# Steps of the next layer's start placed anew in a twelve-layer decoder: keys a round sooner, first scores in the lead, one group inside the layer behind

## The chip, the cores and the metric

The kernel runs on one NeuronCore of a Trainium2 chip, as one program. The metric is the device time of one execution in microseconds (us); of the kernel before there are three runs, and their median counts. Engines in the text: PE (matmul; PEld its weight loads), DVE (vector), ACT (scalar functions), POOL (GpSimd), SP (which issues most transfers).

## The reference, cut to what matters

A decoder with four blocks; each has an attention, a cross attention to a context and a feed-forward part, every one with a layer norm ahead of it and a residual behind it. x is 32 sequences x 128 positions x 128 channels, in float32. So there are twelve layers:

```
x = x + layer(layernorm(x))          # for each of
0  state-space mixer
1  cross attention, 8 heads of 64
2  16 experts, 4 chosen per token
3  causal attention, 16 heads of 8; k, q and v from a latent of 64
4  cross attention, 16 heads of 8, with a key mask and biases
5  8 experts of width 256, 2 chosen; router: silu(x rw1 + rb1) rw2 + rb2
6  attention with one head of 128
7  cross attention, 16 heads of 8, plus a learned bias by relative position
8-11  sparsemax attention, a cross attention, experts
```

Every attention is softmax(q k^T * scale + terms) v, for each sequence by itself.

## The kernel before, in words

**Tiling.** x stays on the chip as eight groups of J = 4 sequences; a group is a tile of 128 positions x 4 x 128. Every layer loops over the eight groups (G = 8). In the attentions a round is one sequence, so a layer has 32 rounds, n = 4 g + j.

**Order of work.** Two things decide it. `Ordered` (L181) wraps PE, DVE and ACT; between `follow(T, A, V)` and `follow()` these engines keep the order of the program text. Outside it, and for POOL and SP always, a scheduler orders what has been written. Since `Ordered` makes the call, most rows of the profile have its line, L194, and are told apart by the names of their tiles. Layers are overlapped by generators: the steps of a coming layer are written as `yield`-separated pieces, and the running layer calls `next` on them at fixed places. `run2(lead3)`, `run3(lead5)`, `run5(bias7, lead7)` and `run7` at the bottom of the program chain them: layer 1 carries layer 2's `front(0)`, layer 2 carries the lead of layers 3 and 4 (which are one call of `attention16` with 64 rounds), these carry layer 5's, and so on.

**attention16** (L492-L622), for layers 3, 4 and 7. `scores(n)`: PE multiplies q by expanded keys into two PSUM tiles `two` (halves, 8 heads each; r = 0 to 3 are quarters of 4 heads), then adds the terms of `extra` (causal or mask) behind all four; DVE takes the maximum of each head (`s<-two`) and subtracts it into SBUF (`bbig<-two,s`). A head quarter with `own` = 1 is not subtracted: ACT's exponent reads PSUM itself, with the maximum as bias, a head at a time. `exponentials(half)` (called e(0), e(1)) are ACT's. `transposes(n, half)`: PE turns the exponents over, ACT copies them out. `weighted(n)`: PE multiplies by the values and by ones; DVE divides. `step(g)` runs the next piece of group g's preparation (norm, turning over, keys, queries, values; written in `layer3`, `layer4` and `layer7`). `expand_keys` (L467) multiplies k, copies it with ACT, and makes four masked copies `gbig<-bmid,cs` on POOL (L477), one for each r. `normed` (L386) is a layer norm whose products are POOL's (L397); `norm` (L334) uses DVE. In a round, `go_round` calls: transposes(n, 0); scores(n+1); transposes(n, 1); e(0); step of group g+1 (and of g+2 in the last round of a group); e(1); weighted(n-1); every fourth time `project`, which adds to x. `run` begins at n = -1, so the first scores of a call are made there. `lead` is five steps of group 0 and one of group 1.

**layer3**: the pieces of a group are the norm, the turning over, the latent (`a1_down`, round j = 1), k and q from the latent (round j = 2), and the values. **layer4**: `own` is (0, 0, 0, 0), scale 8^-0.5 is applied in the exponent.

**layer1** calls `next(then)` in its rounds n = 28 to 31. **layer2** and **layer5** are experts: `front(i)` is the router (norm, product, top choice by `first_k`, weights split in three parts); `by_expert` turns the weights over; `group(i, ...)` is the experts' matmuls. Layer 5's `group` interleaves pieces of `others` after each expert: for group i the one-head attention (layer 6) of group i-1, `one_head(i-1)`; for group 0 it is `bias7`, the splitting and spreading of layer 7's bias table. After group 7, `one_head(7)` runs by itself, interleaved with `lead7`.

Of the kernel before, what the change touches and what calls it, by code (L numbers as in the profile page):

```python
# [10 lines left out]
F32 = mybir.dt.float32  # L11
# [4 lines left out]
ALU = mybir.AluOpType  # L16
# [9 lines left out]
G = 8  # L26
# [178 lines left out]
def program(ctx, tc, cols, x, ctxt, mask, drop, dfirst, dsmall, dwide, drows, dunits, dexperts, dconst, drel, dwq, out):  # L205
# [286 lines left out]
    def attention16(*layers):  # L492
# [91 lines left out]
        def lead():  # L584
            for _ in range(5):
                step(0)
                yield
            step(1)
            yield

        def run(then):
            follow(T, A, V)
            for n in range(-1, groups * J + 2):
                go_round(n, then)
            follow()

        def go_round(n, then):
            g, j = n // J, n % J
            e = None
            if 0 <= n < groups * J:  # L600
                transposes(n, 0)
            if n + 1 < groups * J:
                e = scores(n + 1)
            if 0 <= n < groups * J:
                transposes(n, 1)
            if e:
                e(0)
            if n >= 0:
                step(g + 1)
                if j == 3:  # L610
                    step(g + 2)
                if g + 1 >= groups or (j == 3 and g + 2 == groups):
                    next(then, None)
            if e:
                e(1)
            if 0 < n <= groups * J:
                weighted(n - 1)
            if n > 1 and (n - 2) % J == J - 1:
                done = (n - 2) // J
                project(done % G, outs.pop(done), *layers[done // G][3:5])  # L620
# [12 lines left out]
    def linearT(w, src, bias=None, scale=1.0):  # L633

        p = ps()
        mm(p, w, src)
        o = gmid()
        if bias is not None:
            A.activation(o, p, AF.Identity, bias=bias)
        else:  # L640
            A.mul(o, p, scale)
        return o
# [311 lines left out]
    def layer1(then):  # L954
# [108 lines left out]
        for n in range(last + 1):  # L1063
            i, j = n // J, n % J
            ahead = n + 1 < last
            if n < last:
                if ahead:
                    e0 = scores(n + 1, 0)
                transposes(n, 0)
                if ahead:  # L1070
                    e0[0]()
            if n > 0:
                project_out(n - 1)
            if n < last:
                transposes(n, 1)
                if ahead:
                    e0[1]()
                    e1 = scores(n + 1, 1)
                if j == 1 and i + 1 < G:
                    prepare(i + 1, 1)  # L1080
                if n + 2 < last:
                    project_in(n + 2)
                if ahead:
                    e1[0]()
                    project_values(n + 1)
                    e1[1]()
                weighted(n)
                if j == 0 and 0 < i and i + 1 < G:
                    prepare(i + 1, 0)
                if i == G - 1:  # L1090
                    next(then)
        follow()

# [1 line left out]
    def layer2():  # L1095
# [4 lines left out]
        def front(i):  # L1100

            if i == 0:
                heads["w"] = part_tiles()
            wparts = heads["w"]
            xn = mid.tile([128, J, D], F32, tag="xn", name="xn", bufs=2)
            norm(xg[i], xn)
            yield
            xnT = turned_over(xn)
            yield
            lg = ps((128, J, 16))  # L1110
            for j in range(J):
                mm(lg[:, j, :], xnT[:, j * 128 : (j + 1) * 128], W["f0_gate"])
            sc, sf = small(J, 16), small(J, 16)
            A.activation(sc, lg, AF.Tanh, scale=0.5)
            V.tensor_scalar(sc, sc, 0.5, 0.5, ALU.mult, ALU.add)
            V.tensor_tensor(sf, sc, bc(WW["gate_bias"], 1, J), ALU.add)
            yield

            s4 = sf.rearrange("p j (g e) -> p (j g) e", e=4)
            pairs, gs = small(J * 4, 6), small(J, 4)  # L1120
            V.tensor_tensor(pairs[:, :, 0:3], s4[:, :, 0:3], s4[:, :, 1:4], ALU.add)
            V.tensor_tensor(pairs[:, :, 3:5], s4[:, :, 0:2], s4[:, :, 2:4], ALU.add)
            V.tensor_tensor(pairs[:, :, 5:6], s4[:, :, 0:1], s4[:, :, 3:4], ALU.add)
            V.tensor_reduce(gs.rearrange("p j g -> p (j g)"), pairs, AX.X, ALU.max)
            gm = first_k(gs, 4, 2)

            V.tensor_scalar(gm, gm, 1.0, -NEG, ALU.subtract, ALU.mult)
            V.tensor_tensor(s4, s4, bc(gm.rearrange("p j g -> p (j g)"), 2, 4), ALU.add)
            sel = first_k(sf, 16, 4)
            V.tensor_tensor(sel, sel, sc, ALU.mult)  # L1130
            tot = small(J)
            V.tensor_reduce(tot, sel, AX.X, ALU.add)
            V.tensor_scalar(tot, tot, 1e-20, None, ALU.add)
            V.reciprocal(tot, tot)
            V.tensor_scalar(tot, tot, 2.5, None, ALU.mult)
            V.tensor_tensor(sel, sel, bc(tot, 2, 16), ALU.mult)
            P.tensor_tensor(xg[i], xg[i], xn, ALU.add)
            heads[i] = xnT, part_weights(wparts[i % 2], sel, 16)
            yield
# [46 lines left out]
    def layer3():  # L1186
        def before(i, h):
            xn = normed(i)
            yield
            xnT = turned_over(xn)  # L1190
            yield
            p = ps()
            mm(p[0:64, :], W["a1_down"], xnT)
            lat = gmid((64, 512))
            A.copy(lat, p[0:64, :])
            yield
            h["k"] = expand_keys(W["a1_k"], lat)
            h["q"] = linearT(W["a1_q"], lat)
            yield
            v = values_tile()  # L1200
            pv, f = ps((128, J, 8)), small(J, 8)
            for j in range(J):
                mm(pv[:, j, :], lat[:, j * 128 : (j + 1) * 128], W["a1_v"])
            A.copy(f, pv)
            P.tensor_copy(diagonal(v)[:, 0:J], bc(f, 2, 4))
            h["v"] = lambda j, r, n: flat(v[:, j, n])

        return before, 8**-0.5, lambda i, j, r: ((identb, bc(causal, 1, 4), True),), W["a1_o"], None, None, (0, 0, 0, 1)


    def layer4():
        masks = {}

        def before(i, h):
            mi = gmid((128, J * S), I32)
# [6 lines left out]
            yield  # L1222
            h["k"] = expand_keys(W["x1_Wk"], ctxT[i], W["x1_bk"])
            yield
            h["q"] = linearT(W["x1_Wq"], xnT, W["L1_xattn_bq"])
            yield
            h["v"] = head_values(ctxT[i], W["x1_Wv"], WW["L1_xattn_bv"])

# [1 line left out]
            row = slice(32 * r, 32 * r + 1)  # L1230
            return ((onesb[row, :], bc(masks[i][row, j * S : (j + 1) * S], 1, 4), True),)

        return before, 8**-0.5, extra, W["x1_Wo"], WW["L1_xattn_bo"], None, (0, 0, 0, 0)


    def layer5():
# [3 lines left out]
        def front(i):  # L1240

            if i == 0:
                heads["w"] = part_tiles()
            wparts = heads["w"]
            xn = mid.tile([128, J, D], F32, tag="xn", name="xn", bufs=2)
            norm(xg[i], xn)
            yield
            xnT = turned_over(xn)
            yield
            if i == 0:  # L1250
                yield
                yield
            p = ps()
            mm(p, W["f1_rw1"], xnT)
            hT = gmid()
            A.activation(hT, p, AF.Silu, bias=W["L1_ffn_rb1"])
            lg = ps((128, J, 8))
            for j in range(J):
                mm(lg[:, j, :], hT[:, j * 128 : (j + 1) * 128], W["f1_rw2"])
            yield  # L1260
            l, m = small(J, 8), small(J)
            V.tensor_tensor(l, lg, bc(WW["L1_ffn_rb2"], 1, J), ALU.add)
            sel = first_k(l, 8, 2)
            V.tensor_reduce(m, l, AX.X, ALU.max)
            V.tensor_tensor(l, l, bc(m, 2, 8), ALU.subtract)
# [6 lines left out]
            heads[i] = xnT, part_weights(wparts[i % 2], sel, 8)  # L1272
            yield

        def run(first, then):
            ups = [U[5][:, e * 128 : (e + 1) * 128] for e in range(8)] + [U[6][:, e * 128 : (e + 1) * 128] for e in range(8)]
            downs = [U[6][:, 1024 + e * 128 : 1152 + e * 128] for e in range(4)]
            downs += [U[7][:, e * 128 : (e + 1) * 128] for e in range(12)]
            pick = picks(8)
            eb2 = W["f1_eb2"]  # L1280
            eb2_rest, eb2_parts = bmid((128, 128)), gmid((128, 3, 128), BF16)
            P.memset(eb2_rest, 0.0)
            V.tensor_copy(eb2_rest[0:24, :], eb2)
            parts3(eb2_rest, [eb2_parts[:, n] for n in range(3)])
            wT = by_expert(heads[0][1])
            for i in range(G):
                wT = group(i, wT, ups, downs, pick, eb2_parts, one_head(i - 1) if i else first)
            for _ in one_head(G - 1):
                next(then, None)

        def group(i, wT, ups, downs, pick, eb2_parts, others):
            xnT = heads.pop(i)[0]
# [17 lines left out]
            for e in range(8):  # L1310
# [5 lines left out]
                    for _ in front(i + 1):  # L1316
                        pass
                else:
                    next(others, None)
            for n in range(3):  # L1320
                mm(oT, eb2_parts[:, n], wT, False, n == 2)
            if i + 1 < G:
# [39 lines left out]
                V.scalar_tensor_tensor(xg[i][:, j, :], o[:, j, :], rec[:, j : j + 1], xg[i][:, j, :], ALU.mult, ALU.add)  # L1362
            yield

        return front(0), run


    def layer7():
# [501 lines left out]
    load_units(6, 7)  # L1870
    lead3, run3 = attention16(layer3(), layer4())
    run2(lead3)
    lead5, run5 = layer5()
    run3(lead5)
    load_units(8)
    bias7, layer = layer7()
    lead7, run7 = attention16(layer)
    run5(bias7, lead7)
    run7(iter(()))
    layer8_first()  # L1880
    layer9()

# [31 lines left out]
```

## Time and profile before

| | us |
|---|---|
| three runs: 3094.29, 3098.97, 3100.82; median | 3098.97 |
| the profiled execution, its own time | 3108.52 |
| its span in the profile | 3106.7 |
| layer 3, first to last reciprocal | 1134.4 to 1428.1 |
| layer 4, the same | 1435.6 to 1690.7 |
| layer 7, the same | 2086.5 to 2347.2 |
| layer 5's groups 1 to 6, each, by the ends of the additions to x | 43.2 |

Rows of a timeline give the start, the duration, the engine, the line, the operation, out<-in by tile names, the shape, how many instructions are joined in the row, and in brackets how long the engine had stood idle and which engine ended that. Rows of stretches give the busy time of each engine, and PEclk, the granted clock as a share of full speed (mean over the whole profile: 0.903). A wait is put down to the engine that released it last.

### The profile page before, as it was taken

The numbers are of one execution on the slowest core, as the hardware profiler recorded it, in microseconds if no ns is written. First come the engines' busy times: TensorE is split into PE (matmuls) and PEld (weight loads), VectorE is DVE, ScalarE is ACT, GpSimd is POOL, SyncE is SP. The second block draws the span as 40 slices with busy tenths as digits, with TensorE's granted clock in tenths as the row PEclk, the third lists the DMA queues.
The fourth block names the chain that finished last, engine by engine and source line by source line (L and its number), as shares of the span: only waits on it lengthen the run. The fifth ranks groups of instructions, "written<-read, shape, count | busy, mean of one in ns | idle before, by whom it ended". The sixth has DMA issues, their size and how long they took to land.

```text
span 3106.7 us, 55574 instructions
## 1 busy us (share of the span) xinstructions
PE 2576.8 (83%) x22554; PEld 1651.8 (53%) x22554; DVE 2106.3 (68%) x4228; ACT 1509.0 (49%) x3411; POOL 996.4 (32%) x1034
## 2 busy tenths in 40 slices
PE   4887889999989988888887999978886869886554
PEld 2555556777744445556664444445553657543433
DVE  4776747888788756667877555458895328777883
ACT  3555534444422245556654445447772226555563
POOL 3343332322210122234542000034434355424444
PEclk8888879999989999999999999979997889997777
DMA  3000000000000000000000000000003243100000
GB/s 108 2 2 2 5 19 4 8 8 1 11 11 1 0 31 2 5 8 9 8 5 15 1 1 1 0 1 2 1 2 125 79 150 106 62 18 14 21 11 21
DMA packets 50146, 68.35 MB, mean 22 GB/s; under 512 B 3681, under 2 KB 41570, under 8 KB 49762
## 3 DMA queue, kind: packets, MB, share of 16 engines
q1 hardware_dynamic: 42608, 33.84, 3.5%
q0 software_dynamic: 6848, 27.81, 2.7%
q8 instruction: 178, 2.92, 0.4%
q10 hardware_dynamic: 434, 3.14, 0.3%
q14 instruction: 78, 0.64, 0.1%
HBM read 51.11 MB, written 13.68 MB: 21 GB/s over the span
## 4 chain that ended last, share of the span: by engine, by line
PE 51%; DVE 30%; ACT 7%; POOL 7%; issue 3%; DMA 1%; another core or an unknown queue 1%; SPq 0%; POOLq 0%; DVEq 0%; ACTq 0%
PE ps L194 22%; PE two L194 15%; PE acc L194 14%; DVE bbig L194 12%; DVE s L194 9%; DVE bmid L194 4%; DVE gmid L194 3%; ACT bbig L194 3%; POOL xn L397 3%; POOL gbig L477 2%; ACT bmid L194 2%; POOL s L395 1%; ACT gmid L194 1%; ACT gbig L194 1%; DVE x L194 1%
## 5 line engine op out<-in xcount | busy, mean ns | idle before, releaser
L194 PE MATMUL ps<-cs,bbig 128*128 128x128 f32 x2208 | 330.9, 290 | 77.8 <-ACT bbig L194 43.4
L194 ACT COPY bbig<-ps 128x512 f32<-128x512 f32 x416 | 226.9, 586 | 270.3 <-PE ps L194 270.0
L194 PEld LDWEIGHTS ps<-cs,bbig 128*128 128x128 f32 x2208 | 255.9, 147 | 183.7 <-ACT bbig L194 98.0
L194 DVE TENSOR_REDUCE s<-two 128x8 f32<-128x1024 f32 (+1 forms) x192 | 234.2, 1220 | 143.5 <-PE two L194 142.4
L194 PE MATMUL two<-xnT,u 128*128 128x512 f32 x512 | 264.5, 617 | 14.0 <-DVE bmid L194 7.8
L194 DVE TENSOR_TENSOR bbig<-bbig 128x256 f32<-128x256 f32 (+4 forms) x394 | 274.3, 749 | 2.0 <-ACT bbig L194 1.0
L194 PE MATMUL acc<-bmid,u 128*128 128x512 f32 x448 | 238.5, 619 | 29.6 <-DVE bmid L194 28.2
L194 PE MATMUL two<-gbig,gmid 32*128 32x512 f32 (+1 forms) x1280 | 205.9, 578 | 32.9 <-POOL gbig L477 32.0
L477 POOL TENSOR_SCALAR gbig<-bmid,cs 128x512 f32<-128x512 f32 x96 | 148.6, 1564 | 209.0 <-ACT bmid L194 209.0
L194 DVE TENSOR_TENSOR bmid<-bmid,ps 128x512 f32<-128x512 f32 x192 | 129.9, 684 | 109.1 <-ACT bmid L194 90.3
L194 ACT ACTIVATE bbig<-bbig 128x1024 f32<-128x1024 f32 (+1 forms) x160 | 141.8, 887 | 94.7 <-DVE bbig L194 94.2
L194 ACT ACTIVATE bbig<-two,s 128x256 f32<-128x256 f32 (+1 forms) x384 | 153.9, 439 | 26.9 <-DVE s L194 23.5
L194 ACT ACTIVATE bmid<-two 128x512 f32<-128x512 f32 x104 | 61.7, 596 | 196.3 <-PE two L194 186.4
L194 PEld LDWEIGHTS two<-xnT,u 128*128 128x128 f32 x512 | 92.6, 194 | 119.1 <-issue 55.2
L194 PEld LDWEIGHTS acc<-bmid,u 128*128 128x128 f32 x448 | 80.7, 195 | 130.2 <-DVE bmid L194 72.6
L194 DVE TENSOR_TENSOR bbig<-two,s 128x1024 f32<-128x1024 f32 (+1 forms) x128 | 139.7, 1092 | 8.6
L194 ACT ACTIVATE bmid<-two,ws 128x512 f32<-128x512 f32 x128 | 85.2, 686 | 117.7 <-PE two L194 115.8
L1014 POOL TENSOR_TENSOR bbig<-bbig,s 128x1024 f32<-128x1024 f32 x32 | 60.6, 1893 | 238.6 <-PE two L194 154.4
L194 ACT ACTIVATE bbig<-bbig,s 128x128 f32<-128x128 f32 x384 | 118.8, 388 | 24.2 <-DVE s L194 24.2
L194 PE MATMUL ps<-cs,xn 128*128 128x128 f32 x288 | 66.2, 318 | 72.8 <-ACT xn L194 31.4
L489 POOL MEMSET val<- 128x512 f32 x72 | 39.0, 543 | 260.8 <-PE acc L194 260.0
L194 PEld LDWEIGHTS two<-gbig,gmid 32*128 32x128 f32 (+1 forms) x1280 | 82.0, 191 | 73.9 <-POOL gbig L477 35.2
(291 smaller groups left out, 5976.9 us busy)
## 6 DMA issues: line engine op xcount, KB each, us to landing
u<-in_units SPq DMA_DIRECT2D x10, 768.0 KB
gmid<-in_ctx SPq DMA_DIRECT2D x16, 256.0 KB, 2.6
xs<-bbig SPq DMA_DIRECT2D x4, 903.0 KB, 6.0
xt<-xs SPq DMA_DIRECT2D x28, 129.0 KB, 3.0
x<-in_x SPq DMA_DIRECT2D x8, 256.0 KB, 10.6
gmid<-in_mask SPq DMA_DIRECT2D x8, 256.0 KB, 3.3
ys<-bbig SPq DMA_DIRECT2D x2, 1024.0 KB
gmid<-ys SPq DMA_DIRECT2D x8, 256.0 KB, 5.3
```

Source lines behind the costliest of these rows:

```text
L194: d = f(*args, **kwargs)
L395: P.tensor_tensor(rs, rs, K["nhalf"], ALU.pow)
L397: P.tensor_scalar(xn[:, j, :], xg[i][:, j, :], mv[:, j, 0:1], rs[:, j : j + 1], ALU.subtract, ALU.mult)
L477: P.tensor_scalar(o[:, n, :], k, K["n4"][:, n : n + 1], None, ALU.mult)
L489: P.memset(o, 0.0)
L1014: (V if c2 else P).tensor_tensor(pr[:, four, :], pr[:, four, :], bc(nm[:, four], 2, 256), ALU.mult)
```

## The change

- **Layer 3**: for groups 1 to 7, k and q become a function `late`, kept in `held`, and `go_round` calls it at the end of the round in which the latent is made, after `weighted`.
- **attention16**: `lead` gets a seventh piece, scores(0) with both exponentials; `run` starts at n = 0. `go_round` also calls `next(others)` in each round, after `weighted`.
- **Layer 4**: q is scaled by 8^-0.5 when it is copied (its bias once, in front); the scale of the scores is 1.0; `own` is (0, 0, 0, 1).
- **Layer 1** calls `next(then)` at n = 27 to 30.
- **Layers 2 and 5**: `front(0)` uses `normed`. In layer 5's `front(0)` Silu is replaced by Identity, Tanh and a product on DVE, with the router logits halved in turn; its two empty pieces go; the picks and the parts of the output bias (`setup`) move from `run` into the lead.
- **Layers 5 to 7**: `bias7` runs in group 1 beside `one_head(0)`, `lead7` in group 7 beside `one_head(6)`, and `one_head(7)` is given to `run7` as `others`.

```diff
@@ attention16
             step(1)
             yield
+            e = scores(0)
+            e(0)
+            e(1)
+            yield
 
-        def run(then):
+        def run(others, then):
             follow(T, A, V)
-            for n in range(-1, groups * J + 2):
-                go_round(n, then)
+            for n in range(groups * J + 2):
+                go_round(n, others, then)
             follow()
...
             if 0 < n <= groups * J:
                 weighted(n - 1)
+            if g + 1 < groups and "late" in held[g + 1]:
+                held[g + 1].pop("late")()
+            next(others, None)
@@ linearT
-            A.activation(o, p, AF.Identity, bias=bias)
+            A.activation(o, p, AF.Identity, bias=bias, scale=scale)
@@ layer1
-                if i == G - 1:
+                if n in range(last - 5, last - 1):
                     next(then)
@@ layer2
-            xn = mid.tile([128, J, D], F32, tag="xn", name="xn", bufs=2)
-            norm(xg[i], xn)
+            if i == 0:
+                xn = normed(i)
+            else:
+                xn = mid.tile([128, J, D], F32, tag="xn", name="xn", bufs=2)
+                norm(xg[i], xn)
@@ layer3
-            yield
-            h["k"] = expand_keys(W["a1_k"], lat)
-            h["q"] = linearT(W["a1_q"], lat)
+
+            def late():
+                h["k"] = expand_keys(W["a1_k"], lat)
+                h["q"] = linearT(W["a1_q"], lat)
+
+            if i:
+                h["late"] = late
+            yield
+            if i == 0:
+                late()
             yield
@@ layer4
+        V.tensor_scalar(W["L1_xattn_bq"], W["L1_xattn_bq"], 8**-0.5, None, ALU.mult)
...
-            h["q"] = linearT(W["x1_Wq"], xnT, W["L1_xattn_bq"])
+            h["q"] = linearT(W["x1_Wq"], xnT, W["L1_xattn_bq"], 8**-0.5)
...
-        return before, 8**-0.5, extra, W["x1_Wo"], WW["L1_xattn_bo"], None, (0, 0, 0, 0)
+        return before, 1.0, extra, W["x1_Wo"], WW["L1_xattn_bo"], None, (0, 0, 0, 1)
@@ layer5
-            if i == 0:
-                yield
-                yield
             p = ps()
             mm(p, W["f1_rw1"], xnT)
             hT = gmid()
-            A.activation(hT, p, AF.Silu, bias=W["L1_ffn_rb1"])
+            if i == 0:
+
+                t = bmid()
+                A.activation(hT, p, AF.Identity, bias=W["L1_ffn_rb1"])
+                A.activation(t, hT, AF.Tanh, scale=0.5)
+                yield
+                V.scalar_tensor_tensor(hT, t, 1.0, hT, ALU.add, ALU.mult)
+            else:
+                A.activation(hT, p, AF.Silu, bias=W["L1_ffn_rb1"])
...
+        def lead():
+            yield from front(0)
+            setup()
+            yield
...
             wT = by_expert(heads[0][1])
             for i in range(G):
-                wT = group(i, wT, ups, downs, pick, eb2_parts, one_head(i - 1) if i else first)
-            for _ in one_head(G - 1):
-                next(then, None)
+                others = [one_head(i - 1)] if i else []
+                if i == 1:
+                    others.append(first)
+                if i == G - 1:
+                    others.append(then)
+                wT = group(i, wT, ups, downs, pick, eb2_parts, others)
...
-        return front(0), run
+        return lead(), run, one_head(G - 1)
@@ the end of the program
-    lead5, run5 = layer5()
-    run3(lead5)
+    lead5, run5, last6 = layer5()
+    run3(iter(()), lead5)
...
-    run7(iter(()))
+    run7(last6, iter(()))
```

## The prediction, made before the changed kernel had run

> **What bounds the kernel now.** I read the page first: busy shares, clock row, the chain that ended last.
>
> ```profile
> PE 2576.8 (83%) x22554; PEld 1651.8 (53%) x22554; DVE 2106.3 (68%) x4228; ACT 1509.0 (49%) x3411; POOL 996.4 (32%) x1034
> ...
> PEclk8888879999989999999999999979997889997777
> ...
> PE 51%; DVE 30%; ACT 7%; POOL 7%; issue 3%; DMA 1%; another core or an unknown queue 1%; SPq 0%; POOLq 0%; DVEq 0%; ACTq 0%
> ...
> L477 POOL TENSOR_SCALAR gbig<-bmid,cs 128x512 f32<-128x512 f32 x96 | 148.6, 1564 | 209.0 <-ACT bmid L194 209.0
> ```
>
> No engine is full: PE and DVE hold the chain in turns, DMA hardly appears. So work taken off a busy engine is worth little, and a stretch in which nobody works is worth its length. The last line is a key expansion: four of these make one group's keys, 4 x 1.564 = 6.26 us. I therefore looked at busy time by stretch: layer 3, layer 4, the tail from layer 5's last group to layer 7's first scores, layer 7.
>
> ```profile
> core 0: us, PE busy (x) PEld busy (x) DVE busy (x) ACT busy (x) POOL busy (x), PEclk, DMA share, GB/s
> 1134.00:1428.00 294.00, 249.95 (x3050) 161.58 (x3049) 190.14 (x289) 163.28 (x344) 95.04 (x101) 0.94 0.01 4
> 1435.00:1691.00 256.00, 219.21 (x3010) 149.64 (x3009) 207.53 (x306) 146.98 (x215) 115.14 (x138) 0.94 0.04 11
> 2029.00:2071.00 42.00, 27.07 (x89) 15.46 (x89) 17.76 (x48) 12.13 (x26) 19.69 (x24) 0.66 0.00 0
> ...
> 2086.50:2347.00 260.50, 210.88 (x2860) 142.46 (x2852) 222.84 (x403) 198.57 (x527) 107.06 (x135) 0.94 0.04 13
> ```
>
> Layer 3 has the least DVE work of the three attentions and is the longest. The tail has every engine under 65% and a clock of 0.66. Then the timeline inside a layer 3 group, in rows of one engine each:
>
> ```profile
> 1176.15 1.98 PE L194 MATMUL ps<-gmid,ws 64*128 64x512 f32 x4 [0.24 <-ACT bbig L194]
> ...
> 1178.86 6.19 POOL L477 TENSOR_SCALAR gbig<-bmid,cs 128x512 f32<-128x512 f32 x4 [16.75 <-ACT bmid L194]
> ...
> 1185.11 2.09 PE L194 MATMUL two<-gbig,gmid 32*128 32x512 f32 x8 [4.07 <-POOL gbig L477]
> 1187.13 1.83 PE L194 MATMUL two<-causal,identb 128*128 128x512 bf16 x4
> 1188.20 1.23 DVE L194 TENSOR_REDUCE s<-two 128x8 f32<-128x1024 f32 x1 [6.83 <-PE two L194]
> ...
> 1189.43 1.07 ACT L194 COPY bbig<-ps 128x512 f32<-128x512 f32 x2 [7.66 <-PE ps L194]
> ```
>
> The next group's k product is at 1176.15, POOL gets it at 1178.86 and is done at 1185.05; PE has stood 4.07 us, DVE 6.83, ACT 7.66. After it the scores take 2.09 us against 1.14 for the same eight at 1172.93, the causal terms 1.83 against 1.04. The ends of DVE's reciprocals, one a round, show the size: rounds of a layer 3 group take about 9.9, 13.6, 7.1 and 7.7 us, 38.3 in sum; the second is the stall. It comes at all seven boundaries into groups 1 to 7.
>
> **Part A, layer 3's keys a round sooner.** k and q (4 matmuls, 2 ACT copies, 4 POOL products, for each of 7 groups) go from round j=2 to the end of round j=1; nothing is added. PE: k comes about 7.4 us sooner by the round, some 1.1 us later within it (behind `weighted`, 1.08 + 1.06 us of matmuls), so POOL ends about 6 us sooner against a stall of 4.07: about 2 us to spare. Its wait for the latent, copied by ACT in the same round, lies beside `weighted`. On POOL's queue the products pass no long work: what follows them is the 0.54 us clearing of the value tile. What is late next is the chain of one round: reduce 1.22, subtraction 1.23, reduce 1.22, subtraction 0.69, small 0.16 on DVE, exponents 0.63 + 1.12 on ACT, then the scores that reuse that PSUM and the next reduce, 1.7: about 7.9. The k and q work of 2 us and its copies still go into some round, so I take 8.3 for the long one: 7 x (13.57 - 8.3) = 36.9. Check from the other side: stall 4.07 + slow matmuls (0.95 + 0.79) = 5.81, x 7 = 40.7. I take **-37**, range -28 to -44.
>
> A rule speaks against this. The Trainium skill, SBUF: State Buffer, section "Who interferes with whom": a DVE instruction with two SBUF inputs and a GpSimd instruction that reads SBUF exclude each other for the whole instruction. Before, DVE stood idle during most of the 6.2 us of POOL; now it works through them. Were each group to pay the full 6.2, 7 x 6.2 = 43 us would eat A. The trace has the overlap elsewhere: in layer 4 the 128x1024 subtraction took 1.225 us when a key expansion ran (13 times) and 1.224 when none did (45), in layer 7 the 512 one 0.692 and 0.690; the POOL op stayed at 1.56 in all three. These operands lie partly in PSUM, so the rows hold for this kernel's forms: price 0.
>
> **Part B, layer 3's first scores** (and both exponentials) inside `lead`. Its scores were already early (1106 to 1110, before layer 2's end at 1110.7); what goes is a 1.28 us table load and the transposes' wait for it (PE 4.57 to 5.06 us idle at 1116), of which most is add_out's own. **-1.5** (-4 to 0).
>
> **Part C, layer 1 to 2**: `next` a round earlier and the first norm's products on POOL (4 x 0.78 us, row of L397) instead of DVE. The norm costs a round of 17.7 against 11.6 now; moving it gives back 4 to 5. But in the build's order the selection block (about 13 us of DVE at 866 to 881) then comes ahead of the last round's copies out of PSUM and only two of four expert up-blocks stand before it. **0** (-6 to +6).
>
> **Part D, layer 4's last four heads** read PSUM with the bias in the exponent. DVE: 1.23 becomes 0.69 + 0.16, -0.38 a round. ACT: 1.06 becomes 0.63 + 1.12, +0.69. PSUM half 1 is free not at the subtraction's end but after ACT's last exponent, about 1.2 us later; queued behind the wait on PE are scores r = 2, 3, the masks (which come after all scores), transposes and `weighted`, and DVE's next reduce waits for them. So no round is under some 7.8 us. Layer 4's rounds are about 8.5, 7.6, 7.1 to 9.0, 7.1 to 8.0: the short ones gain up to 1.7 a group, the long ones lose DVE time. Nearest row: layer 3, which has this form. **+5** (-4 to +13).
>
> **Part E, layer 4 to 5**: Silu becomes Identity + Tanh (0.6 + 0.6 us) and a DVE product of 0.69; the table load of 1.28 us at 1670.6 goes, the two empty steps too, and the setup moves ahead. In before the expert weights are turned over only at 1689.9, after 4.6 to 5.4 us of idle PE waiting for DVE. I count -6 for these turned over sooner, -2 for the round the empty steps burdened, +1.2 for ACT, +2 for the router product waiting for DVE's new op; the 8.2 us splitting of the bias table (1671 to 1687) still lies in the same DVE block. **-5** (-10 to +2). Layer 7's bias table, begun in group 1 instead of 0, only moves PE work between two full groups: 0.
>
> **Part F, the tail.** From layer 5's last matmul (2028.9) to the first reciprocal of layer 7 (2086.5) are 57.5 us, one chain of small steps:
>
> ```profile
> 2034.12 1.25 PE L194 MATMUL ps<-cs,gmid 128*128 128x128 f32 x4 [3.78 <-DVE gmid L194]
> ...
> 2052.34 3.11 POOL L477 TENSOR_SCALAR gbig<-bmid,cs 128x512 f32<-128x512 f32 x2 [10.81 <-ACT bmid L194]
> ...
> 2058.59 1.56 PE L194 MATMUL two<-gbig,gmid 32*128 32x512 f32 x6 [3.55 <-POOL gbig L477]
> ...
> 2060.17 1.22 DVE L194 TENSOR_TENSOR bbig<-two,gbig 128x1024 f32<-128x1024 f32 x1 [5.39 <-PE two L194]
> ```
>
> Each row has waited for one other engine: PE 3.78 us for a norm, POOL 10.81 for a copy of k, PE 3.55 for keys, DVE 5.39 for scores. Of the 57.5, two rounds of layer 7 itself are 2 x 8.6 = 17.2, and about 5 stay (add_out, first transposes). The rest, 35, goes: one-head group 7's serial steps and layer 7's lead. But the work comes back: lead's 5 us of PE (products at 1.06 each and first scores 1.61) into group 7, which at 43.2 us a group is PE's; the one-head group (9.5 PE, 5.7 DVE, 3.8 ACT) into rounds 0 to 5, where DVE has 222.8 of 260.5 us: +6. 57.5 - 17.2 - 5 - 5 - 6 = 24.3: **-24** (-32 to -12).
>
> **Sum**: -37 - 1.5 + 0 + 5 - 5 - 24 = -62.5. The profiled execution took 3108.52 (span 3106.7), so 3046.0; it lies 9.6 above the median of the runs, 3098.97, and from that the same sum gives 3036.5.
>
> **Rivals.**
> 1. *The stall only moves.* If the keys still arrive late, or PE's own 7 us a round plus steps become the bound, A gives 15, not 37: 3036.5 + 22 = 3058. For: PE is 250 of 294 us busy in layer 3. Against: at full clock those 250 lose the 1.7 us of slow matmuls a group, and 2 us are to spare.
> 2. *The tail stays.* If the one-head steps break layer 7's rounds (each step waits for ACT and holds PE, and behind it the scores) F gives 4: 3036.5 + 20 = 3056. For: DVE's 86% there; each step has a PE-ACT-PE dependency. Against: six steps stand a whole round apart.
> 3. *All covers hold*: A -43, D 0, E -8, F -30, B and C -4: -85, 3014.
> 4. *Slower: layer 4's PSUM.* Every score of 32 rounds waits for ACT. To undo the 67.5 of the other parts the wait must cost 67.5/32 = 2.1 us a round, that is, rounds of 10.1 instead of 8.0. At 2.4 us it is +77, in sum 3099 + 9 = 3108. Against: layer 3, same form, has rounds of 7.1 and 7.7.
> That the change doesn't do what it says is excluded for A (the order shows k and q ahead of the next transposes); for C it is in the range.
>
> **How the numbers follow.** Forecast 0.58, rival 1 0.14, rival 2 0.14, rival 3 0.10, rival 4 0.02, little change by some sum of these 0.02. A measurement tells about 0.2% (6 us): faster 0.96, same 0.02, slower 0.02. Likeliest 3036; range from a little beyond rival 3 to a little beyond rivals 1 and 2: 3008 to 3068.
>
> **What would show it.** A: no wait of PE for POOL's key products in layer 3, rounds of 8 to 9.5, group sums about 33, no half-clock after the boundary. F: last matmul of group 7 to first reciprocal about 25 us, layer 7 about 6 us longer. D: layer 4's PE waits for ACT at scores, span 256 to about 261. E: expert weights' turn sooner against the last masks. Wrong if layer 3's group sums stay above 35.5, if layer 4 grows by over 13, or if layer 7's rounds grow by over 2 us each in 0 to 5.

## The result, and the profile after

The changed kernel takes 3060.78 us (median of four runs, 3048.22 to 3068.78) against 3098.18 for the kernel before, run beside it: a ratio of 0.9877, interval 0.9841 to 0.9912, 37 us less. A gain of 62 was forecast. The profiled execution is the slowest of the four, 3068.78 with a span of 3066.8, so the stages below are taken from spans: 3106.7 to 3066.8, -39.9.

The page after, the same two lines as before and the key products:

```profile
PE 2563.0 (84%) x22535; PEld 1638.7 (53%) x22554; DVE 2086.1 (68%) x4254; ACT 1529.3 (50%) x3540; POOL 1007.4 (33%) x1042
...
PE 49%; DVE 31%; ACT 8%; POOL 6%; issue 3%; DMA 1%; another core or an unknown queue 1%; SPq 0%; POOLq 0%; DVEq 0%; ACTq 0%
...
L477 POOL TENSOR_SCALAR gbig<-bmid,cs 128x512 f32<-128x512 f32 x96 | 148.7, 1564 | 160.0 <-ACT bmid L194 160.0
```

Hardly a share has moved, and the chain is as mixed as it was: the page says that no engine lost much work, not where 40 us went. For that the span has to be cut at the same events in both traces (ends of the additions to x, and of the reciprocals, one a round):

| stretch | before | after | difference | forecast |
|---|---|---|---|---|
| start to layer 1's group 6 | 823.4 | 828.6 | +5.2 | 0 |
| layer 1's group 7, layer 2, to layer 3's first round (B, C) | 310.9 | 302.9 | -8.0 | -1.5 |
| layer 3, rounds (A) | 293.8 | 264.8 | -29.0 | -37 |
| layer 3 to 4 | 7.4 | 6.7 | -0.8 | 0 |
| layer 4, and layer 5's groups 0 and 1 (D, E) | 338.3 | 338.2 | -0.1 | 0 (+5 and -5) |
| layer 5's groups 2 to 6 | 217.4 | 219.7 | +2.3 | 0 |
| layer 5's group 7 (F) | 39.8 | 48.3 | +8.5 | +5 |
| from there to layer 7's first round (F) | 55.4 | 19.6 | -35.8 | -35 |
| layer 7, rounds (F) | 260.7 | 282.0 | +21.2 | +6 |
| the rest | 759.6 | 756.0 | -3.6 | 0 |

The first and the last row are not the change's: in eleven further programs, whose layer 0 and last layers are the same, layer 0 with layer 1's first group ends between 528.6 and 545.2 us, and the rest takes 734.4 to 745.0.

The same stretches by engine, first layer 3, then the start of layer 7, then the whole of its rounds:

```profile
1131.50:1396.50 265.00, 244.66 (x3059) 157.84 (x3061) 185.99 (x292) 165.53 (x352) 95.22 (x101) 1.00 0.02 5
...
2028.80:2080.00 51.20, 43.12 (x412) 28.92 (x412) 30.95 (x53) 30.89 (x80) 15.01 (x20) 0.77 0.00 1
2028.80:2311.00 282.20, 231.19 (x2905) 156.10 (x2905) 226.14 (x414) 203.37 (x534) 107.60 (x135) 0.90 0.03 12
```

And the start of layer 7 before the change, of the same number of rounds:

```profile
2086.50:2119.60 33.10, 27.40 (x372) 18.39 (x364) 28.91 (x48) 27.02 (x73) 14.92 (x20) 0.95 0.01 2
```

In layer 3 the clock is full now (0.94 before) and PE is 92% busy. In layer 7 the first four rounds take 51.2 us instead of 33.1. PE's busy time in them has gone from 27.4 to 43.1, DVE's from 28.9 to 31.0: what fills these 18 us is PE, at a clock of 0.77 instead of 0.95.

**Layer 3, a group after.** The rows of the timeline round the new place of k and q:

```profile
1197.03 1.06 PE L194 MATMUL acc<-bbig,cs 128*32 128x128 f32 x32
...
1198.55 1.45 PE L194 MATMUL ps<-gmid,ws 64*128 64x512 f32 x3
1198.85 0.87 ACT L194 ACTIVATE bbig<-two,s 128x128 f32<-128x128 f32 x3
...
1199.60 0.60 ACT L194 COPY bmid<-ps 128x512 f32<-128x512 f32 x1
1200.07 0.63 ACT L194 ACTIVATE gmid<-ps 128x512 f32<-128x512 f32 x1
1200.25 1.16 PE L194 MATMUL ps<-ws,gmid 128*128 128x128 f32 x8 [0.26 <-ACT bmid L194]
1200.30 6.19 POOL L477 TENSOR_SCALAR gbig<-bmid,cs 128x512 f32<-128x512 f32 x4 [10.18 <-ACT bmid L194]
...
1202.85 1.14 PE L194 MATMUL two<-gbig,gmid 32*128 32x512 f32 x8
...
1209.28 1.13 PE L194 MATMUL two<-gbig,gmid 32*128 32x512 f32 x4
```

The same place before the change, where k and q did not yet stand there:

```profile
1169.03 1.06 PE L194 MATMUL acc<-bbig,cs 128*32 128x128 f32 x32
...
1172.93 1.14 PE L194 MATMUL two<-gbig,gmid 32*128 32x512 f32 x8
```

POOL is done at 1206.49, and the first scores that use its keys, those of the next group's first sequence, come at 1209.28 without a wait for it: 2.8 us to spare here and at five more boundaries, 1.3 at the first, where I had 2. No wait of PE for POOL's key products is left in the layer. But k and q now stand last in the round, and the transposes and scores of the next round stand behind them: from the end of `weighted` (its last row is `acc<-bbig,cs`) to the next scores are 4.76 us, where they were 2.84. Most of the 1.92 us more is the PE work of k and q (1.98); 0.26 is the wait of the next product (1200.25) for the PSUM tile that the copy of k sets free. The rounds of a group are 10.80, 8.89, 7.12 and 7.71 instead of 9.93, 13.54, 7.12 and 7.71.

**Layer 7, second round after.** What fills it:

```profile
2030.25 1.12 PE L194 MATMUL ps<-cs,bbig 128*128 128x128 f32 x4 [1.81 <-ACT gmid L194]
2031.30 2.09 PE L194 MATMUL two<-gbig,gmid 32*128 32x512 f32 x8
...
2038.51 1.98 PE L194 MATMUL ps<-gmid,ws 128*128 128x512 f32 x4
...
2041.81 0.49 PE L194 MATMUL ps<-ws,gmid 128*128 128x128 f32 x2 [1.31 <-ACT gmid L194]
2042.22 0.48 PE L194 MATMUL ps<-wr,cs 1*128 1x128 f32 x2
...
2046.05 0.79 PE L194 MATMUL ps<-wr,cs 1*128 1x128 f32 x2
2046.77 1.97 PE L194 MATMUL ps<-cs,bbig 128*128 128x128 f32 x8
...
2050.86 1.23 DVE L194 TENSOR_TENSOR bbig<-two,gbig 128x1024 f32<-128x1024 f32 x1 [10.25 <-PE two L194]
```

This is the piece of `one_head(7)` that makes q, k and v. From 2038.51 to 2046.77, 8.3 us, PE works for it or waits for its copies (1.31 us); the next round's transposes and scores stand behind it, and DVE idles 10.25 us. The same two matmuls take 0.48 us at 2042.2 and 0.79 at 2046.1: in between, the granted clock fell from 1.0 to 0.5, here called half clock. The round took 18.50 us.

### The profile page after: what moved, and what is told of

It reads as the page before. It is cut to its first block, busy times and chain, and to the rows that moved or that the text cites. A ratio compares the mean times of both kernels' runs of the same rounds, so it can differ in the third digit from the quotient of the medians.

```text
span 3066.8 us, 55735 instructions
## 1 busy us (share of the span) xinstructions
PE 2563.0 (84%) x22535; PEld 1638.7 (53%) x22554; DVE 2086.1 (68%) x4254; ACT 1529.3 (50%) x3540; POOL 1007.4 (33%) x1042
## 4 chain that ended last, share of the span: by engine, by line
PE 49%; DVE 31%; ACT 8%; POOL 6%; issue 3%; DMA 1%; another core or an unknown queue 1%; SPq 0%; POOLq 0%; DVEq 0%; ACTq 0%
PE ps L194 22%; PE two L194 15%; PE acc L194 13%; DVE bbig L194 13%; DVE s L194 9%; DVE bmid L194 4%; DVE gmid L194 3%; ACT bbig L194 3%; POOL xn L397 3%; ACT bmid L194 2%; ACT gmid L194 1%; DVE x L194 1%; POOL s L395 1%; ACT gbig L194 1%; POOL s L364 1%
## 5 line engine op out<-in xcount | busy, mean ns | idle before, releaser
L194 PE MATMUL two<-gbig,gmid 32*128 32x512 f32 (+1 forms) x1280 | 223.1, 570 | 3.1 <-ACT bbig L194 2.4
L194 ACT ACTIVATE bbig<-two,s 128x256 f32<-128x256 f32 (+1 forms) x512 | 189.7, 419 | 24.5 <-DVE s L194 21.2
L194 ACT ACTIVATE bbig<-bbig 128x512 f32<-128x512 f32 (+1 forms) x160 | 128.1, 801 | 86.6 <-DVE bbig L194 86.1
L194 ACT ACTIVATE bbig<-bbig,s 128x128 f32<-128x128 f32 x384 | 118.7, 387 | 27.4 <-DVE s L194 27.4
L194 DVE TENSOR_TENSOR bbig<-two,s 128x1024 f32<-128x1024 f32 (+1 forms) x128 | 122.6, 958 | 8.6
L194 ACT COPY bbig<-bbig 128x256 f32<-128x256 f32 (+3 forms) x320 | 97.8, 375 | 49.2 <-DVE bbig L194 47.2
```

What stands on the lines that cost most here:

```text
L194: d = f(*args, **kwargs)
```

## The experiments

Two theories to begin with. One: the one-head pieces take back in layer 7's rounds nearly all that the tail gives, since PE, not DVE, carries them, and they wait for ACT. Two, the rival: the tail's gain stands, and layer 7's slow start has another cause (the new lead, a chance state of the clock). Four kernels were run beside each other.

**The changed kernel again**, and the **tail as before**:

```diff
@@ e2, against the changed kernel
-                if i == G - 1:
-                    others.append(then)
                 wT = group(i, wT, ups, downs, pick, eb2_parts, others)
+            for _ in one_head(G - 1):
+                next(then, None)
+            for _ in then:
+                pass
-        return lead(), run, one_head(G - 1)
+        return lead(), run, iter(())
```

> The changed kernel once more, beside the others. Both theories: 3060 within 8. The first four rounds of layer 7 took 11.5, 18.5, 9.9 and 11.4 us in its profile against 7.6 to 8.9 before, with half of that stretch at half clock. If this is the one-head pieces' doing, the rounds are slow in this profile too; if it is a chance state of the clock, the rounds may be 8 to 9 us here and the time near the fastest run, 3048.

> The changed kernel, but group 7's one-head steps run by themselves after layer 5, beside layer 7's lead, as before. Theory 1 (the one-head pieces hold up layer 7's rounds and take back nearly all that the tail gives): the tail is 55 us again, layer 7's rounds 8 to 9 us, in sum 3064. Theory 2 (the tail's gain stands and the slow rounds have another cause, such as the new lead): layer 7 stays at 280 us and the sum is 3085.

Again: ratio 0.9869 (0.9842 to 0.9897), 3044.64 against 3082.43; the first rounds of layer 7 are slow again, 10.1, 18.1, 10.3 and 9.6. Tail as before: ratio 0.9883 (0.9855 to 0.9911), 2.9 us over it. From the end of layer 5's group 6 to the end of layer 7's rounds it is 346.7 us in the changed kernel's second profile, 349.9 in its first, and 349.8 with the tail as before. Three further kernels below that have the changed tail show 345.7, 348.3 and 349.6. So moving the one-head pieces and the lead is worth 0 to 4 us. It is theory 1.

**One-head steps alone** behind layer 5, the lead in group 7 as changed (in e2's diff the loop is `for _ in one_head(G - 1): pass`, and `others.append(then)` stays):

> Layer 7's lead in layer 5's group 7 as changed, but the one-head steps of group 7 right behind layer 5 and outside layer 7's rounds. Theory 1: layer 7 back to 261 us (-21), the tail longer by the one-head chain, 15 to 20 us: 3055 to 3060. Theory 2: layer 7 stays near 280 and the tail grows as well: 3078.

Ratio 0.9885 (0.9857 to 0.9912). Layer 7 is back at 261.6, the way to its first round is 41.2 and group 7 takes 48.3. This splits F. The lead moved into group 7 (e2 to e3): the way 50.6 to 41.2, group 7 from 38.3 to 48.3, nothing won. The pieces moved into the rounds (e3 to e1): the way 41.2 to 18.2 (-23), layer 7 from 261.6 to 278.5 (+17), and the medians 3.3 apart.

**Pieces ahead of the second exponents**:

```diff
+            next(others, None)
             if e:
                 e(1)
             if 0 < n <= groups * J:
                 weighted(n - 1)
...
-            next(others, None)
```

> The one-head pieces ahead of the second exponents of the round instead of at its end, so that ACT's copy of a piece is queued before them and the PSUM tile is free sooner. Theory 1: the 1.8 us in which PE waits for this copy at each of the six pieces goes, and some of the half clock: 3048 or less. Theory 2: no effect, 3060.

Ratio 0.9836 (0.9812 to 0.9860), 9.9 us under e1 in the medians. Its profile shows less of it: 344.1 for the stretch above, hardly below the 345.7 to 349.9 of the kernels with the pieces at the round's end, with a first round of 19.2. PE waits for ACT in another place: the copies of layer 7's own step and of the piece come behind eight exponents of 2.45 us. The direction rests on the run times of these four kernels alone, and the size stays open, since their intervals overlap a little.

Next question: is it the half clock at layer 7's start that makes the pieces dear? **Pieces from round 5 on**:

```diff
-            next(others, None)
+            if n > 4:
+                next(others, None)
```

> The changed kernel with the one-head pieces in layer 7's rounds 5 to 10 instead of 0 to 5. Theory 1a (the pieces are dear because they meet the half clock of layer 7's start; at full clock the q, k, v piece takes some 4.5 us of PE instead of 8.4): rounds 0 to 3 back to 8 to 9 us, rounds 5 to 10 longer by 8 in sum, layer 7 about 269, the time 8 to 10 us under the changed kernel's, ratio to before near 0.984. Theory 1b (the waits for ACT's copies and the PSUM tile are the cost, at any clock): the same 17 to 20 us, only later, ratio 0.987.

Ratio 0.9881 (0.9857 to 0.9905). Rounds 0 to 3 are 7.6, 8.9, 8.8 and 8.0, as before the change; the next four take 14.9, 11.2, 15.6 and 9.9, and layer 7 281.8 in all. Theory 1a falls: the pieces bring the half clock with them.

```profile
2061.09 1.11 PE L194 MATMUL ps<-cs,bbig 128*128 128x128 f32 x4 [1.87 <-ACT bbig L194]
2062.14 2.09 PE L194 MATMUL two<-gbig,gmid 32*128 32x512 f32 x8
...
2067.93 1.11 PE L194 MATMUL ps<-cs,bbig 128*128 128x128 f32 x4 [3.11 <-DVE x L194]
...
2086.14 0.49 PE L194 MATMUL ps<-ws,gmid 128*128 128x128 f32 x2 [1.50 <-ACT gmid L194]
...
2089.72 0.79 PE L194 MATMUL ps<-wr,cs 1*128 1x128 f32 x2
```

These are its rows: PE waits of 1.87, 3.11 and 1.50 us come with the pieces (the second through DVE, which the norm of the piece holds up), and the scores behind the first take 2.09 us instead of 1.14.

**Each other part by itself.** Keys only (A on the kernel before), layer 4 as before (D undone), router as before (E undone):

```diff
@@ e6, against the kernel before: layer3's late() as in the change, and in go_round
             if 0 < n <= groups * J:
                 weighted(n - 1)
+            if 0 <= n and g + 1 < groups and "late" in held[g + 1]:
+                held[g + 1].pop("late")()
@@ e7, against the changed kernel
-        V.tensor_scalar(W["L1_xattn_bq"], W["L1_xattn_bq"], 8**-0.5, None, ALU.mult)
...
-        return before, 1.0, extra, W["x1_Wo"], WW["L1_xattn_bo"], None, (0, 0, 0, 1)
+        return before, 8**-0.5, extra, W["x1_Wo"], WW["L1_xattn_bo"], None, (0, 0, 0, 0)
@@ e8, against the changed kernel: layer 5's front, setup and bias7 as before
-                others = [one_head(i - 1)] if i else []
-                if i == 1:
-                    others.append(first)
+                others = [one_head(i - 1) if i else first]
                 if i == G - 1:
                     others.append(then)
...
-        return lead(), run, one_head(G - 1)
+        return front(0), run, one_head(G - 1)
```

> The kernel before with layer 3's keys and queries a round sooner and nothing else. If the parts add up, layer 3's rounds take 265 us as in the changed kernel (-29) and the time is 29 less than before, ratio 0.9906; that is most of what the whole change gave. The rival, that the other parts gave as much as the keys: -15 or less, ratio 0.995.

Ratio 0.9920 (0.9897 to 0.9942): some 25 us; layer 3's rounds 266.0, -27.7. The keys are most of the change, as the first case has it.

> The changed kernel with layer 4's last four heads subtracted on DVE as before. By the changed profile (224.0 to 219.4 us in groups 0 to 6) the form with the bias in the exponent gained 4.6, so +4 to +5 against the changed kernel, groups 0 to 6 at 224. By the prediction's reasoning (the PSUM tile comes free later) it would have cost 5: -5.

Ratio 0.9882 (0.9859 to 0.9906), which can't be told from the changed kernel's. In the profile groups 0 to 6 of layer 4 take 221.3 us against 219.4, but group 6 already holds pieces of the router. Groups 0 to 5 take 187.8 or 187.9 us with the new form (router as before included; 186.2 and 186.3 in the two kernels below with the query elsewhere) and 190.6 to 190.9 without it (the kernel before and the keys-only one included). So the form with the bias gains about 3, not 4.6 and not -5; the whole layer says the same (257.6 against 254.5).

> The changed kernel with layer 5's first router, its setup and layer 7's bias table placed as before (Silu, table load, two empty pieces; bias table in group 0). By the prediction this costs 5. By the changed profile (from round 28 of layer 4 to layer 5's group 1 it went from 114.2 to 118.8 us, with the bias table's work in it both times) it gains up to 4: 3 to 5 us under the changed kernel.

Ratio 0.9857 (0.9833 to 0.9881). From layer 4's first round to the end of layer 5's group 1 its profile shows 338.0 us, the changed one 338.2, and kernels with the new router 336.9 too. The new router is worth about nothing. Nor is e8's whole lead over the changed kernel shown to be the router's.

**Can the measured terms be had back?** The query back in round j=2, the keys as changed; the pieces earlier and q, k, v in three; both, with the old router:

```diff
@@ e9
             def late():
                 h["k"] = expand_keys(W["a1_k"], lat)
-                h["q"] = linearT(W["a1_q"], lat)
...
             if i == 0:
                 late()
+            h["q"] = linearT(W["a1_q"], lat)
             yield
@@ e10, with e4's edit
             qT = linearT(W["a2_wq"], xnT, W["L2_attn_bq"])
+            if i == G - 1:
+                yield
             kT = linearT(W["a2_wk"], xnT, W["L2_attn_bk"])
+            if i == G - 1:
+                yield
             pv = ps((128, J, 128))
```

> The changed kernel with only layer 3's keys at the end of round j=1; the queries stay in round j=2 as before. If the keys alone cleared the stall and the queries' product, copy and PSUM tile at the round's end are what made the round 10.8 instead of 9.9 us: that round about 9.9, the next about the same 8.9, layer 3 6 us shorter, 3 to 6 us less in all. If the work is only moved to the next round: the same 265.

Ratio 0.9838 (0.9810 to 0.9866). Layer 3's rounds are 9.8, 8.7, 7.1 and 7.7, the layer 257.2 instead of 264.8: -7.6, and the forecast's -37 is nearly there: 293.8 to 257.2 is -36.6, of which about 1.2 comes with other parts, since the keys-only kernel has 266.0 where the changed one has 264.8. From `weighted` to the next scores are 3.58 us instead of 4.76. The query's place at the round's end was what A lacked.

```profile
1122.80:1380.00 257.20, 243.77 (x3059) 157.59 (x3062) 186.42 (x291) 165.32 (x352) 95.23 (x101) 1.00 0.02 5
```

PE is busy 95% of layer 3 in it: little is left there but PE's own work.

> The changed kernel with the one-head pieces ahead of the second exponents, and the q, k, v piece of the last group cut in three (eight pieces in rounds 0 to 7). If that one piece's 8.4 us of PE and its waits for two copies are the longest step: the worst round about 12 instead of 18 to 19 us, layer 7 at 270 or less, ratio to before 0.982. If each piece costs its wait wherever it stands: 276 as with the earlier pieces alone, ratio 0.984 or more.

Ratio 0.9837 (0.9810 to 0.9864). The worst round is 14.1 instead of 18 to 19, but the layer still takes 274.7. The rows of that round show why:

```profile
2053.53 0.79 PE L194 MATMUL ps<-wr,cs 1*128 1x128 f32 x2
2054.25 0.80 PE L194 MATMUL ps<-ws,gmid 128*128 128x128 f32 x2
...
2057.87 0.79 PE L194 MATMUL ps<-wr,cs 1*128 1x128 f32 x2
2058.59 1.94 PE L194 MATMUL acc<-bbig,val 128*32 128x128 f32 x32
...
2062.16 1.87 PE L194 MATMUL ps<-cs,bbig 128*128 128x128 f32 x8
```

The v matmuls alone run from 2053.2 to 2058.6 at half clock, and what follows them runs at half clock too. Smaller pieces spread the same PE work; they don't cover it. The expectation of 270 was missed, that of 276 about met.

> Both of the above with layer 5's router and layer 7's bias table placed as before. If the parts add up: 3 to 6 us for the queries, 10 to 14 for the pieces, 0 to 3 for the router, ratio to before about 0.981, under both kernels.

Ratio 0.9814 (0.9787 to 0.9841), 3029.44 against 3090.65: the fastest kernel of the study, faster than before by 61 us and, by the ratios, than the changed kernel by about 0.6%, though its interval touches that of the first result. In its profile layer 3 has 257.2 and layer 7 275.0.

## Why the prediction was off, point by point

The time lay in the range, towards its upper end, and the sign was right. The sum was 25 us too good in the run times. That it was not worse is in part luck: B, C and D gave about 14 us more than forecast and made up for A and E, which gave 13 less, so that the miss is about F's.

- **A**: right in mechanism, the stall is gone. Its size, -37, was -29.0. The failed term is "I take 8.3 for the long one" with the other rounds as they were: the long round became 8.89, and the round that took the work in grew from 9.93 to 10.80. Of the k and q products, 2 us of PE, I had charged the long round 0.4 and the other nothing. At the end of the round they cost 1.92 us ahead of the next scores, nearly their full time; the query alone cost next to nothing in round j=2, as the experiment with it there (-36.6) shows. The keys-only kernel has -27.7 for A by itself. My 2 us to spare were right (2.8).
- **The shared port**, priced at 0: right, but it was not against the rule. The Trainium skill, SBUF — State Buffer, "Who interferes with whom", speaks of DVE instructions with two SBUF inputs, and says that one with at most one SBUF input does not contend with GpSimd, "outside the 2-port perf modes", of which a `tensor_tensor` has none. The subtraction `bbig<-two,s` has one, as its scores are in PSUM. Of my two rows layer 7's is no test: `bbig<-bbig,s` has no input in PSUM, but POOL's key product overlaps only its last 0.12 us. In layer 3 after, the 128x1024 subtraction takes 1.226 us when POOL makes keys (8 times) and 1.225 when not (23), the products 1.56 as ever.
- **B and C**: -8.0 instead of -1.5. Layer 1's last group went from 58.06 to 55.21 us, and the way from there to layer 3's first round from 252.9 to 247.7. I had let the order of the selection block eat the 4 to 5 us that I had found; it didn't. The keys-only kernel, which has neither part, needs 311.0 us for the whole stretch, the ten other kernels of the experiments 302.3 to 303.0. B and C were not run apart, but by events C's part (layer 1's last group and layer 2's first) is 5.7 us shorter and B's (from layer 2's group 6 on) 2.2: B about as forecast, C not.
- **D**: +5 forecast, about -3 measured by undoing it. Of layer 4's rounds the second did grow, from 7.6 to 8.6, as forecast; but the fourth fell from 7.1 to 8.0 to 6.7, and most third rounds of 8.4 to 9.0 to 7.2. The term that failed is "no round is under some 7.8 us": the third and the fourth are.
- **E**: -5 forecast, about 0. The expert weights are turned over 26.0 us after the last masks instead of 27.7: 1.7 sooner, not 6. The new DVE product held PE's router matmuls 1.47 us, as ACT's Silu had held them 1.36 before, and the weighted sums behind them ran at half clock both times (1.94 us, at 1632.4 and at 1673.8 before).
- **F**: -24 forecast, -6.1 in the two profiles, and of these the pieces and lead themselves are 0 to 4 by undoing them; the rest is there without them, the way being 50.6 instead of 55.4 us, in the kernels whose lead makes the first scores. The tail went as forecast (-35.8 against -35). The term that failed is "+6" for the one-head group in layer 7's rounds: it was +21.2 (17 in the second profile). I took DVE for the bound there, because it was 86% busy, and charged its 5.7 us. But DVE, PE and ACT wait for each other in turn within a round, so an added piece is not hidden under the busiest one: its 9.5 us of PE stand in the chain, with waits of its own, and PE is at half clock more often: PE's busy time in four rounds grew by 15.7 us.

Rival 2 said this ("each step waits for ACT and holds PE, and behind it the scores"; F worth 4, 3056 in all) and had 0.14. It should have had more than the forecast: that each piece takes a product from PE to ACT and back to PE could be read in the code, and its PE time was in my own sum, only not charged.

How much of layer 7's 17 to 21 us is the clock and how much plain work can be read in part. The kernel with layer 4 as before has the same layer 7, pieces included, but its clock fell less there:

```profile
2025.70:2300.70 275.00, 222.04 (x2904) 149.99 (x2904) 225.18 (x412) 202.80 (x533) 106.69 (x135) 0.93 0.04 12
```

At a clock of 0.93, against 0.94 before the change, layer 7 takes 14.3 us more than before, with a second round of 17.4; at the changed kernel's 0.90 it takes 21. So some 14 us are the pieces' work and waits, and some 7 went with the clock. This is an estimate: the clock differed by chance, and no run set it.

## What to carry to other kernels

In this pipeline, whose engines wait for each other in turn, none at 100%, a step that was moved in cost its full time on PE or more (1.9 of 2.0 us for k and q, 14 and more for the one-head pieces with 9.5), even where DVE was the busiest on average; cut such a step out of one place only if the other has a real gap. When a producer is moved ahead to clear a stall, look at what now stands behind it; put only the late operand (here the keys) early, and leave the rest where it was free. And keep the undo of each part: two of six parts (E, and the moved pieces and lead of F) gave little or nothing.

## What the runs showed of the hardware that had not been expected

PE's clock fell without PE standing idle for long. By the trace's record of the granted clock, around the start of the changed kernel's layer 7 it went to half at 2008.8, 2019.0, 2029.2 and 2042.9 us; in the 3.41 us ahead of these PE had been busy 0.9, 2.0, 1.0 and 2.1 us. The Trainium skill, TensorE: Matmul & The Clock Gate, Part 1: The HAM clock gate, puts the fall after an idle window of about 3.4 us; here windows that were up to 62% busy were followed by it. After the last of them PE worked without a gap and stayed at half clock for 10.2 us.
